# Earlier ring loads before a recurrent scan, and two of eight additions moved from VectorE to ScalarE and Pool after it

## The chip, the core and the metric

The kernel runs on one core of one Trainium2 chip. The metric is the device time of one execution in microseconds; lower is better. All data is float32.

## What is computed

The input x has 16 images of 128 channels and 64 x 64 pixels. Two layers follow each other, and each adds its result to its input:

```
x = x + lstm(gn(x))        # layer 0: gn = group norm over 32 groups of 4 channels
x = x + quantum(gn(x))     # layer 1

lstm:    skew the rows (row i shifted right by i), then scan over columns:
         gates = w_is @ x_t + w_ss0 @ h_of_the_row_above + w_ss1 @ h
         o, f, i = sigmoid(...); g = tanh(...)
         c = f*c + i*g;  h = o*tanh(c);  unskew h
quantum: per pixel: 4 angles = pre_w @ x + pre_b
         state of 4 qubits from cos/sin of the angles, a fixed circuit,
         z_w = sum of squared amplitudes with signs;  out = post_w @ z + post_b
```

## The kernel before

Channels are the 128 partitions. Forty of the 64 rows of all 16 images stay on chip in one tensor, `ring` (10 blocks of 4 rows per image); 24 rows have to be stored and read again, in a DRAM tensor `low`.

**Stage 1, loading and statistics (0 to 117 us).** A loop over the 16 images (line 360) issues on SP's queue two loads into `ring` (lines 362 to 366: 8 blocks and 2 blocks, 1 MB and 0.25 MB) and three loads of 0.25 MB for the other 24 rows into `rest` tiles (line 370; the pool has four buffers). VectorE (DVE) makes statistics pieces of 512 columns (line 373: five from `ring`, then three from `rest`) and one aggregate per image (line 374). Loads on SP and pieces on DVE are executed in the order of the program, so the loads of image b+1 stand behind the rest loads of image b, and a rest load waits until DVE has read the tile four loads before it. Beside this, on PE, ScalarE (ACT) and Pool, runs a chain of 27 small recurrent steps (`inv_step`, lines 184 to 204), which needs no image. When the last aggregate is there, mean and variance of the groups are made with two small matmuls and some operations of 16 columns, and the scan starts.

**Stage 2, the scan (117 to 1305 us).** PE-bound diagonal steps; the order of all engines is the order of the program. Rows that are finished are stored to `low` and replaced in `ring`. At its end the statistics of layer 1 are made.

**Stage 3, layer 1 (from 1320 us).** An image is eight chunks of 512 columns: k = 0 to 2 are low rows, loaded by Pool's queue (`load`, L741) into a pool with 11 buffers, k = 3 to 7 are views of `ring`. The order of every engine is again that of the program, over images b:

```
            load(b + 3)
            po = outputs(b, 0)
            finish(b, 0, po)
            angles(b + 2)
            po = outputs(b, 1)
            squares(b + 1)
            finish(b, 1, po)
```

`angles` makes phases with 16 matmuls that use the array in four column strips (theta, L752), adds a bias on ACT (y, L762), rounds and subtracts on DVE (L763, L764) and takes the sine on ACT in place (L765). The tile y has two buffers, so y of image b+2 takes the place of y of image b. `squares` multiplies the sines by amplitudes (am, L772) and squares them on ACT (sq, L774). `outputs` makes four products per half image in four row strips of the array (po, L781), each in a PSUM bank of its own; a bank has one buffer, so products of the next half wait until `finish` has read the bank. `finish` adds product, bias and input on DVE in place (L798), and SP's queue stores the chunks (L800 low rows, L803 ring rows).

PE executes phases, products and amplitude matmuls in this order: po of half 0 of b, theta of b+2, po of half 1 of b, am of b+1.

## Time and profile before

| | |
|---|---|
| median of three runs (lowest, highest) | 1481.57 us (1478.03, 1482.80) |
| the profiled execution, own time | 1480.57 us |
| its span from first to last instruction | 1478.8 us |
| last aggregate of stage 1 ends | 112.5 us |
| last of the 27 small steps (its copies on Pool end) | 102.4 us |
| first phases matmul of layer 1 | 1320.56 us |
| last addition of layer 1 ends | 1473.35 us |
| mean granted TensorE clock | 0.981 of full speed |

Busy time in the stage of layer 1 (1320 to 1479 us): the additions at L798 take 55.4 + 33.0 us on DVE (128 of them, 743 ns each when alone, 0.68 to 0.69 us apart when they follow one another), y, sine and squares 11.0 + 10.1 + 17.3 us on ACT; Pool issues low loads only (0.54 us each). A low-row load lands 3.7 us after its issue (median), a low-row store 5.2, a 1 MB ring load 8.0.

How to read it: the profile is of one execution. Its rows name the line of the kernel, the engine, the written and read tensors, the count and the busy time. "Idle before" is time in which the engine waited, with what ended the wait. SPq is the queue of transfers issued by SP. "Issue" in the chain of waits is time in which an engine waited for nothing that the profile shows.

### The profile page before, as it was taken

Reading aid. Unit: us, or ns where it says so; the run is one execution under the profiler, and the core shown is the slowest. Engines: PE = TensorE matmul, PEld = TensorE weight load, DVE = VectorE, ACT = ScalarE, POOL = GpSimd, SP = SyncE. Lnnn points to the kernel's source line nnn. Section 1 sums busy time; section 2 is a strip of 40 time slices with the busy share of each in tenths; the row PEclk is TensorE's granted clock in tenths of the full one; section 3 lists DMA queues with packets and bytes.
Section 4 is the critical chain, followed back from the end, with each engine's and each line's share of the span. In section 5 each row is a group of like instructions: output and inputs, shape, how many; then the busy total and the mean of one; then the engine's idle time right before and its main releaser. Section 6 shows DMA issues by size and latency. Waiting matters only on the chain. (4 is left out here: it accounts for less than half of the span.)

```text
span 1478.8 us, 19436 instructions
## 1 busy us (share of the span) xinstructions
PE 1374.0 (93%) x5798; PEld 973.1 (66%) x5798; DVE 976.4 (66%) x2458; ACT 764.6 (52%) x1862; POOL 889.8 (60%) x1694
## 2 busy tenths in 40 slices
PE   4647999999999999999999999999999999859997
PEld 3647888777677667667776776776677787833322
DVE  5884565556665666887777675555555678767775
ACT  3544566556555555555555555555555565432221
POOL 1114778766677667788887776676676666521110
PEclk9999999999999999999999999999999999979987
DMA  8990000000000000133344000000000000028997
GB/s 287 334 313 1 1 2 0 1 0 1 1 0 1 1 1 1 58 114 114 121 139 138 3 1 0 1 1 1 1 1 1 1 1 2 1 79 288 318 318 249
DMA packets 86192, 106.99 MB, mean 72 GB/s; under 512 B 4024, under 2 KB 70728, under 8 KB 86088
## 3 DMA queue, kind: packets, MB, share of 16 engines
q1 hardware_dynamic: 80576, 92.29, 18.3%
q0 software_dynamic: 3840, 12.59, 2.7%
q8 instruction: 46, 0.75, 0.2%
q10 hardware_dynamic: 1672, 0.89, 0.2%
q14 instruction: 58, 0.48, 0.1%
HBM read 59.61 MB, written 46.14 MB: 72 GB/s over the span
## 5 line engine op out<-in xcount | busy, mean ns | idle before, releaser
L483 PE MATMUL ps<-xn,wxT 128*128 128x512 f32 (+18 forms) x1280 | 480.7, 518 | 2.0 <-POOL xn L475 2.0
L596 DVE TENSOR_TENSOR ps<-ps,both 128x256 f32<-128x256 f32 (+9 forms) x544 | 219.7, 408 | 325.7 <-PE ps L574 320.1
L600 ACT ACTIVATE ps<-ps,bias 128x512 f32<-128x512 f32 (+23 forms) x480 | 268.3, 581 | 253.1 <-DVE ps L596 213.3
L483 PEld LDWEIGHTS ps<-xn,wxT 128*128 128x128 f32 x1280 | 231.9, 191 | 174.5 <-issue 155.5
L625 ACT COPY both<-ps 128x256 f32<-128x256 f32 (+9 forms) x544 | 191.4, 355 | 178.7 <-PE ps L574 159.0
L574 PE MATMUL ps<-diff,w1T 128*128 128x256 f32 (+14 forms) x1088 | 283.7, 363 | 0.0
L574 PE MATMUL ps<-diff,w0T 128*128 128x256 f32 (+14 forms) x1088 | 283.2, 362 | 0.0
L516 POOL TENSOR_TENSOR ring<-ring,hst 128x256 f32<-128x256 f32 (+8 forms) x488 | 247.2, 538 | 24.7 <-DVE hst L664 24.7
L574 PEld LDWEIGHTS ps<-hst,wsT 128*128 128x128 f32 x1088 | 195.9, 190 | 85.5 <-DVE hst L664 35.4
L574 PE MATMUL ps<-hst,wsT 128*128 128x256 f32 (+14 forms) x1088 | 241.3, 365 | 5.7 <-DVE hst L664 4.3
L574 PEld LDWEIGHTS ps<-diff,w0T 128*128 128x128 f32 x1088 | 199.7, 190 | 21.1
L574 PEld LDWEIGHTS ps<-diff,w1T 128*128 128x128 f32 x1088 | 199.3, 190 | 20.8
L475 POOL TENSOR_TENSOR xn<-xn,rstd 128x512 f32<-128x512 f32 (+10 forms) x160 | 170.7, 1067 | 15.2 <-DVE rstd L152 2.7
L470 POOL TENSOR_TENSOR xn<-ring 128x256 f32<-128x256 f32 (+8 forms) x213 | 146.9, 699 | 0.0
L664 DVE TENSOR_TENSOR hst<-g,ps 128x256 f32<-128x256 f32 (+13 forms) x320 | 108.4, 369 | 45.0 <-ACT g L655 41.8
L465 POOL TENSOR_TENSOR xn<-ring,mean 128x16 f32<-128x16 f32 (+8 forms) x247 | 130.3, 537 | 12.2 <-DVE mean L138 11.0
L655 ACT ACTIVATE g<-cst 128x256 f32<-128x256 f32 (+20 forms) x320 | 103.0, 368 | 63.8 <-DVE cst L654 63.3
L507 POOL TENSOR_TENSOR diff<-hst 128x240 f32<-128x240 f32 (+9 forms) x136 | 103.0, 757 | 39.0 <-DVE hst L664 35.6
L654 DVE TENSOR_TENSOR cst<-cst,ps 128x256 f32<-128x256 f32 (+20 forms) x320 | 104.6, 368 | 5.5
L651 DVE TENSOR_TENSOR ps<-ps,g 128x512 f32<-128x512 f32 (+20 forms) x160 | 95.2, 595 | 19.1 <-ACT g L600 17.8
L677 POOL COPY edge<-hst 128x16 f32<-128x16 f32 x64 | 25.1, 392 | 136.1 <-DVE hst L664 136.1
L644 DVE TENSOR_TENSOR cst<-cst,ps 128x512 f32<-128x512 f32 (+20 forms) x160 | 92.8, 580 | 16.8 <-ACT ps L600 9.4
(149 smaller groups left out, 1232.1 us busy)
## 6 DMA issues: line engine op xcount, KB each, us to landing
ring<-in_x_dram SPq DMA_DIRECT2D x16, 1024.0 KB, 8.0
out_dram<-ring SPq DMA_DIRECT2D x16, 1024.0 KB, 5.2
rest<-in_x_dram SPq DMA_DIRECT2D x48, 256.0 KB, 5.4
low<-ring SPq DMA_DIRECT2D x6, 2048.0 KB, 7.5
ring<-in_x_dram SPq DMA_DIRECT2D x6, 2048.0 KB, 8.2
low<-low POOLq DMA_DIRECT2D x48, 256.0 KB, 3.7
out_dram<-low SPq DMA_DIRECT2D x48, 256.0 KB, 5.2
ring<-in_x_dram SPq DMA_DIRECT2D x16, 256.0 KB, 8.1
```

Source lines behind the costliest of these rows:

```text
L465: nc.gpsimd.tensor_sub(by_pairs(xn, 0, j, n), x0, over(mean1, n))
L470: nc.gpsimd.tensor_sub(by_pairs(xn, 1, j, n), lower, of)
L475: nc.gpsimd.tensor_mul(v, v, r)
L483: nc.tensor.matmul(ps[g][:, :, a:b], lhsT=wxT[:, g * 128 : (g + 1) * 128], rhs=xns[t % 2][:, :, a:b], start=True, stop=True,)
L507: nc.gpsimd.tensor_sub(diff[:, 0, a1:b], now[:, 1, a1 - NB : b - NB], now[:, 0, a1:b])
L516: nc.gpsimd.tensor_add(x1, x1, by_pairs(new, q, j, n))
L574: nc.tensor.matmul(out, lhsT=w[:, g * 128 : (g + 1) * 128], rhs=rhs, start=False, stop=True, skip_group_check=True,)
L596: nc.vector.tensor_add(v, v, both[g][:, a:b])
L600: nc.scalar.activation(to[:, :, a:w], ps[g][:, :, a:w], FUNC[g], bias=bias[:, g : g + 1])
L625: nc.scalar.copy(both[g][:, a:b], ps[g][:, 0, a:b])
L654: nc.vector.tensor_add(c[:, q], c[:, q], ig[:, q])
L664: nc.vector.tensor_mul(new[:, q, a:v], th[:, q, a:v], act[GO][:, q, a:v])
```

## The change

Stage 1: the two ring loads of an image become a function `rows(b)`. Images 0 and 1 are loaded ahead of the loop, and iteration b loads the ring rows of image b+2 ahead of the rest tiles of image b.

Layer 1: in each half image the addition with j = 3 is split. ACT adds the bias and moves the product from PSUM to a new tile `part` (one buffer), and Pool adds it to the input in place. The pool of low rows gets a twelfth buffer. To make room, the square of half 1 is written into the y tile of its image in place of a tile of its own; both amplitude matmuls are issued ahead of both squares.

```diff
+            def rows(b):
                 n = SLOTS * NW
                 for k0, k1, at in ((AHEAD // ROWS, RING // ROWS, 0), (0, AHEAD // ROWS, n)):
                     nc.sync.dma_start(
                         out=ring[:, k0:k1, b, :],
                         in_=xv[b, :, at : at + (k1 - k0) * BLOCK].rearrange("c (k n) -> c k n", n=BLOCK),
                     )
+            rows(0)
+            rows(1)
+            for b in range(NB):
+                if b + 2 < NB:
+                    rows(b + 2)
                 of = [ring[:, k : k + 2, b, :] for k in range(0, RING // ROWS, 2)]
...
-    lowp = ctx.enter_context(tc.tile_pool(name="lowp", bufs=11))
+    lowp = ctx.enter_context(tc.tile_pool(name="lowp", bufs=12))
     trp = ctx.enter_context(tc.tile_pool(name="trp", bufs=2))
+    partp = ctx.enter_context(tc.tile_pool(name="partp", bufs=1))
...
     def squares(b):
         sqs[b] = []
+        ams = []
         for h in range(2):
             am = ps_a.tile([P, CHUNK], F32, name=f"am{b}_{h}", tag=f"am{h}")
             nc.tensor.matmul(am, lhsT=w_amp[:, h, :], rhs=turns[b], start=True, stop=True)
-            s = trp.tile([P, CHUNK], F32, name=f"sq{b}_{h}", tag=f"sq{h}")
+            ams.append(am)
+        for h, am in enumerate(ams):
+            s = trp.tile([P, CHUNK], F32, name=f"sq{b}", tag="sq") if h == 0 else turns[b]
             nc.scalar.activation(s, am, AF.Square)
             sqs[b].append(s)
...
-            nc.vector.scalar_tensor_tensor(x1, y, b_out, x1, ALU.add, ALU.add)
+            if j < 3:
+                nc.vector.scalar_tensor_tensor(x1, y, b_out, x1, ALU.add, ALU.add)
+            else:
+                part = partp.tile([P, CHUNK], F32, name=f"part{b}_{h}", tag="part")
+                nc.scalar.activation(part, po[j], AF.Identity, bias=b_out)
+                v = part
+                if k >= NT:
+                    v = v.rearrange("p (k n) -> p k n", n=BLOCK)
+                nc.gpsimd.tensor_add(x1, x1, v)
```

More of the change, by code (lines that the diff above doesn't have):

```diff
@@ L359 @@
             done = 0
-            for b in range(NB):
+            def rows(b):
                 n = SLOTS * NW
```

## The prediction

> **What bounds the kernel now.** I read the 40 slices first, then for each of the two changed stages the waits and the chain.

> ```profile
> PE   4647999999999999999999999999999999859997
> DVE  5884565556665666887777675555555678767775
> DMA  8990000000000000133344000000000000028997
> GB/s 287 334 313 1 1 2 0 1 0 1 1 0 1 1 1 1 58 114 114 121 139 138 3 1 0 1 1 1 1 1 1 1 1 2 1 79 288 318 318 249
> ```

> A slice is 37 us. There are three stages: loading with statistics (three slices, transfers at 8 to 9 tenths), the scan (PE at 9, nothing changed there), and layer 1 from 1320 us (PE and transfers both at 9). A gain in the first stage starts the scan earlier and is worth its full length.

> First stage: the waits of SP's queue up to 130 us, the waits of the engines up to 115 us, and three stretches (the last two columns are the share of the transfer engines and GB/s).

> ```profile
> SPq L370 <- DVE stats L373: 35.9, 29, 3.5
> SPq L370 <- DMA rest<-in_x_dram: 12.1, 12, 1.5
> ...
> DVE stats L373 <- DMA ring<-in_x_dram: 24.8, 15, 6.9
> ...
> 9.00:12.00 3.00, 0.49 (x1) 0.20 (x1) 2.04 (x9) 0.81 (x1) 0.00 (x0) 1.00 0.66 175
> 24.00:27.00 3.00, 1.87 (x8) 1.27 (x7) 2.96 (x7) 1.85 (x9) 0.58 (x3) 1.00 0.69 187
> 54.00:69.00 15.00, 9.85 (x44) 9.43 (x44) 12.66 (x23) 8.09 (x32) 3.02 (x16) 1.00 1.08 371
> ```

> DVE waits for ring rows, SP waits with its next load until DVE has read a rest tile, and so the transfers dip: 175 or 187 GB/s against 371 when nothing starves them. The mean from 2 to 108 us is 324.

> Layer 1: one image of the chain of waits, then the waits, then windows [...] (the clock is the column before the transfer share).

> ```profile
> 1396.16 0.70 ACT y L762
> ...
> 1396.88 0.71 DVE theta L763
> ...
> 1397.61 0.70 DVE y L764
> ...
> 1398.35 0.51 issue
> 1398.86 0.59 ACT sq L774
> 1399.45 0.04 issue
> 1399.49 2.68 PE po L781 x8
> 1402.17 3.60 PE theta L752 x16
> ...
> ACT y L762 <- PE theta L752: 77.6, 15, 6.6
> PEld theta L752 <- DMA low<-low: 5.7, 6, 1.3
> ...
> 1354.13:1357.54 3.41, 2.92 (x10) 1.05 (x8) 3.41 (x6) 1.36 (x3) 1.36 (x3) 1.00 0.80 245
> 1357.54:1360.95 3.41, 3.41 (x17) 0.60 (x16) 1.59 (x3) 0.00 (x0) 0.00 (x0) 0.50 0.93 327
> ```

> The chain closes on itself through PE, ACT and DVE: y, its rounding, its sine ("issue" 0.51), the squares, the output products, the next phases, the next y. With a full clock it takes 7.95 us (y at 1361.33 and 1369.28). From y of image 3 (1341.35) to y of image 15 (1453.20) there are 12 periods of 9.32 on average. Seven of them hold a half-clock stretch and average 9.87. Late low rows cost only 5.7 us of weight-load wait in all.

> [...] its half stretches last 3.41 us. But here the window before a half one isn't idle: it is PE busy 2.92 of 3.41, only with the quarter-array output products. In all seven cases the preceding window held those products and at most 0.5 us of other matmuls; with 0.6 us or more the clock stayed full. [...] The trace has 1067 ns for a 128x512 product on Pool (L475) and 580 to 595 on DVE. [...] y is an identity too, and it alternates with the sine with no load after 1318 us.

> **Part 1: ring rows two images ahead.** No instruction is added. On SP's queue 32 ring loads move ahead of the rest loads of two images. The lead keeps 1.3 MB or more queued while SP waits for DVE. Nothing else uses SP here except ACT's weight loads beside it, which share the transfer engines. It has a price: an image's last rest tile lands one 1.3 MB block later relative to the ring rows, so at the end DVE still has images 13, 14 and 15 to finish. Best case: 33.6 MB of x and 0.8 of weights, less the 2.4 of the three last rests, is 32.0 MB; at 0.371 MB/us (row 54:69) and 2.3 us of start that is 88.6 us; 0.7 for a rest tile; then DVE's pieces. From the timeline, five ring pieces take 3.06 us, three rest pieces 1.86, the aggregate 0.37: 2.2 for image 13 and 5.3 each for 14 and 15, 12.8 in all. End 102.1, where the profile has 112.5. DVE alone gives the same: its first rest tile lands at 2.3 + 5.5/0.371 = 17.1, then 2.2 + 15 x 5.3 + some 3 us of small operations, 101.8. Worst case: the mean rate of 30 to 105 us, 0.338, gives 110; delayed weight loads could eat the rest. The chain of 27 single-column steps (L184 to L204) ends at 102.4 and was hidden by 10 us; that cover goes, so it is late next. Gain from -1 to 10. I take 106, which allows for some dips and for the chain slipping: **-6.5 us**.

> **Part 2: layer 1.** Take s as the start of y (the activation at L762) of image b+2.

> Added wait. The second square now overwrites the y tile of image b, which the second output products of b read. There are two y tiles, so y of b+2 may be written only after those products, not after the phases. PE issues them right behind the phases: 1369.06 to 1370.20, and y would start 0.16 later, at 1370.36 instead of 1369.28: +1.08. Behind y on ACT wait its sine, both squares and the new activation; DVE's rounding waits too.

> Removed work. DVE does six additions instead of eight. Before: subtraction ends s+2.13, four additions of 0.68 to s+4.77, the last products (1.06 alone) end and the phases start at s+5.87. After: DVE's three end s+4.09. ACT has sine to 2.79, squares to 3.29 and 3.76, then the new activation, 0.58 like a pipelined y, to about 4.3. Products to 5.4: -0.47. The two matmuls ahead of both squares change nothing, since PE ran them before the squares already.

> Period: phases 5.4 to 7.26, second products to 8.36, y at **8.52** against 7.95.

> Pool. Per image two additions of 1.07 (bounds 0.59, DVE's price, and 1.3) and three issues of low loads, 1.65 together: 3.8 of 8.5 us, hidden. The load of b+4 is now queued behind the second addition of b (s+5.4). The twelfth buffer makes it need only image b's stores, which land near s+4, so it scarcely waits; the rows are needed near s+14 plus. Low waits (2.8 us within the 12 periods) go. On SP the stores of ring rows leave 0.7 to 1 us later, hidden except at the end.

> Clock. Between the end of the full-array products (L772) and the phases lay 3.07 us. Now those products end at s+1.93 and the phases start at 5.4: 3.47[...]. So windows with quarter-array work alone become more likely, and the half stretch then covers phases and second products, which are both on the chain: +1.71. 8.52 + 1.71 = 10.23 is three windows (10.24), so the next period meets the same window again: it locks. Forecast: 12 x 10.24 = 122.9 against 111.85, **+11.0**.

> Before those 12, y of image 2 waits for the second products of image 0, +1.3, and the next period +0.6: **+1.9**. End: from y of image 15, the products of image 14 no longer queue behind two of eight additions (L772 starts at s+7.6, not 9.46: -1.85), but the last addition is 0.65 on ACT plus 1.07 on Pool instead of 0.75, with one DVE turn saved: **-1.45**.

> Sum: -6.5 + 11.0 + 1.9 - 1.45 = **+5.0**. The profiled execution took 1480.57 (span 1478.8, 1.8 around it), 1.0 under the median of 1481.57; the difference put on the median gives 1486.5.

> **Rivals.**
> A, not slower: the clock doesn't lock. With n of 12 periods throttled layer 1 costs 12 x 8.52 + 1.71 n - 111.85 + 0.45, and the whole is -15.7 + 1.71 n. The point is n = 9: at 7, as now, -3.7 (1478); at 3, -10.5 (1471). For it: before, never more than three throttled periods in a row, and a spread from 9.33 to 10.37 us in them. Against: before, 9.87 wasn't a multiple of the window; 10.23 is.
> B, slower yet: the loads ahead bring nothing. SP already waited 12.1 us for earlier transfers to land (12 times), which may hold it again, or DVE's 12.8 us at the end take what the transfers give. Then +11.5: 1493. For it: DVE has 5.3 us of work per image against 5.75 of transfer. Against: the 371 GB/s stretch.
> C: Pool's queue, if stores land late. The load holds the addition behind it, and this holds ScalarE's single part tile: 0.5 us per image, +6 on top: 1492. Against: 4 us of slack.

> **Numbers.** Forecast 0.45, A 0.33, B and C 0.22. A change of 0.3% (4.4 us) is about what can be told from none. The forecast's own range, 1481 to 1491, gives 0.27 slower and 0.18 same; A 0.20 faster and 0.13 same; B and C 0.22 slower. Range 1473 to 1495.

> **What would show it.** First stage: the last aggregate at 106 (112.5 now), no 3 us stretch under 250 GB/s between 12 and 90 us, SP still waiting for DVE. Layer 1: ACT's y released by po (L781), no longer by theta; periods of 8.5 at full clock and 10.2 with a half stretch, eight or more of the latter; no theta wait on low. Pool's addition near 1.07. I am wrong if y starts while second products run, if layer 1's periods fall under 9.2, or if the scan's start moves by under 3 us.

## The result and the profile after

The changed kernel takes 1488.57 us (median of six runs, 1488.00 to 1490.19), the kernel before 1482.01 in the same comparison (also six runs): ratio 1.005, 95% interval 1.0037 to 1.0062. It is slower by 0.5%, on the forecast side; 1486.5 was predicted, with a range to 1495. The profiled execution took 1488.39 us, its span is 1486.6 (before: 1480.57 and 1478.8).

Lines of the page first: the same slices as before, then the new group.

```profile
PE   4658999999999999999999999999999998768886
DVE  6974565566656667877777765555555787755554
DMA  9970000000000000244431000000000000047877
GB/s 313 371 245 1 2 1 1 1 1 1 1 1 1 1 1 1 94 134 133 140 125 57 1 1 1 1 0 1 0 1 1 1 1 1 19 139 274 294 270 250
...
L820 POOL TENSOR_TENSOR ring<-ring,part 128x512 f32<-128x512 f32 x32 | 40.8, 1275 | 115.2 <-ACT part L816 115.1
```

The first two slices move more (313 and 371 GB/s for 287 and 334), so the third has less left to do. The slices of layer 1 move less (274 to 294 for 318) and PE falls to 8 tenths and below: layer 1 has become slower, and not for lack of transfers. An addition on Pool takes 1275 ns.

The first stage: waits of SP's queue up to 130 us, of DVE up to 115 us, and the stretch of 15 us that was the undisturbed one before, with three later ones. A line of waits gives the total in us, how often, and the longest. A line of a stretch gives its length, the busy time of PE, PE's weight loads, DVE, ACT and Pool (with the number of instructions), the granted clock, the share of the transfer engines and GB/s.

```profile
SPq L378 <- DVE stats L381: 27.3, 32, 4.6
SPq L378 <- DMA rest<-in_x_dram: 18.5, 14, 2.2
...
DVE stats L381 <- DMA ring<-in_x_dram: 12.6, 13, 6.9
...
54.00:69.00 15.00, 9.33 (x40) 8.90 (x40) 13.74 (x24) 8.07 (x32) 3.19 (x17) 1.00 1.06 366
93.00:96.00 3.00, 1.97 (x10) 1.89 (x10) 2.89 (x5) 1.54 (x6) 0.57 (x3) 1.00 0.73 279
96.00:99.00 3.00, 1.97 (x10) 1.89 (x10) 3.00 (x7) 1.54 (x6) 0.58 (x3) 1.00 0.63 194
99.00:102.00 3.00, 1.28 (x6) 1.19 (x6) 2.10 (x5) 2.27 (x7) 0.88 (x5) 1.00 0.75 230
```

SP still waits for DVE, but with ring rows queued that wait costs little: from 30 to 90 us the transfers run at 372 GB/s (339 before). From 93 us only rest tiles are left, one at a time behind DVE, and the rate falls. DVE is busy up to 100.4 us and then waits 1.2 us in all for the last rest tiles. The last aggregate ends at 104.0 us instead of 112.5, the 27 small steps end at 101.6, and y of image 0 starts at 1315.79 instead of 1324.23: 8.44 us earlier.

Layer 1: one period of the chain of waits, then the waits of the engines, and stretches of 3.41 us with the granted clock in each. "Half window" stands for such a stretch in which the granted clock is 0.50, "window" for any of them: in both profiles the steps of the clock in layer 1 lie whole multiples of 3.41 us apart (before, half windows start at 1347.30, 1357.54, 1401.91, 1412.15, 1422.39, 1439.46 and 1449.70).

```profile
1377.91 0.70 ACT y L771
...
1378.63 0.71 DVE theta L772
...
1379.42 0.70 DVE y L773
...
1380.15 0.63 ACT y L774
1380.78 0.49 ACT sq L787
1381.27 0.04 issue
1381.31 2.22 PE po L794 x8
1383.53 3.46 PE theta L761 x16
1386.99 1.19 PE po L794 x8
...
ACT y L771 <- PE po L794: 50.9, 14, 3.8
...
1379.93:1383.34 3.41, 2.03 (x8) 0.99 (x8) 3.03 (x6) 2.18 (x4) 0.94 (x1) 1.00 0.79 297
1383.34:1386.75 3.41, 3.41 (x17) 0.59 (x16) 1.20 (x2) 0.69 (x1) 3.17 (x5) 0.50 0.61 177
...
1390.17:1393.58 3.41, 1.96 (x8) 0.99 (x8) 3.03 (x6) 2.18 (x4) 0.87 (x1) 1.00 0.81 306
1393.58:1396.99 3.41, 3.41 (x18) 0.59 (x16) 1.26 (x2) 0.69 (x1) 3.23 (x5) 0.50 0.60 172
```

The second output products (1.19 us) now lie on the chain between the phases and the next y, and y's releaser is po where it was theta. The phases take 3.46 us instead of the 1.92 at a full clock (from 1322.88), because a half window (the 0.50) covers them. The half windows come one in every period: thirteen of them start from 1332.14 to 1455.02 us, 10.24 us apart, three windows. The window ahead of each holds output products and at most 0.32 us of phases or amplitude matmuls; every other window of these images has over 1.9 us of them. From the last amplitude matmul of an image to the next phases, with output products as the only matmuls between, it takes 3.7 to 4.2 us in these periods, 3.0 to 3.1 in most of before; the expectations below call this the stretch without full-array work. The twelve periods from y of image 3 to y of image 15 are all 10.30 to 10.34.

### The profile page after: what moved, and what is told of

Same layout as the page of the kernel before. It is cut to its first block, busy times and chain, and to the rows that moved or that the text cites. A ratio compares the mean times of both kernels' runs of the same rounds, so it can differ in the third digit from the quotient of the medians.

```text
span 1486.6 us, 19469 instructions
## 1 busy us (share of the span) xinstructions
PE 1371.5 (92%) x5798; PEld 973.2 (65%) x5798; DVE 955.4 (64%) x2426; ACT 784.6 (53%) x1894; POOL 929.9 (63%) x1726
## 5 line engine op out<-in xcount | busy, mean ns | idle before, releaser
L582 PEld LDWEIGHTS ps<-diff,w1T 128*128 128x128 f32 x1088 | 199.6, 191 | 20.5
L483 POOL TENSOR_TENSOR xn<-xn,rstd 128x512 f32<-128x512 f32 (+10 forms) x160 | 170.7, 1067 | 15.2 <-DVE rstd L152 2.7
L820 POOL TENSOR_TENSOR ring<-ring,part 128x512 f32<-128x512 f32 x32 | 40.8, 1275 | 115.2 <-ACT part L816 115.1
```

The source lines that it names most:

```text
L483: nc.gpsimd.tensor_mul(v, v, r)
L582: nc.tensor.matmul(out, lhsT=w[:, g * 128 : (g + 1) * 128], rhs=rhs, start=False, stop=True, skip_group_check=True,)
```

## The experiments

Times are medians; ratios are to the kernel before, run beside them. "Twelve periods" means the mean distance of y from image 3 to image 15 in the profiled execution: 9.32 us before, 10.31 after.

| kernel | us | ratio, 95% interval | twelve periods |
|---|---|---|---|
| after | 1488.57 | 1.0037 to 1.0062 | 10.31 |
| ring loads ahead alone | 1472.40 | 0.9914 to 0.9958 | 9.22 |
| layer 1 alone | 1496.23 | 1.0083 to 1.0137 | 10.28 |
| after, full-array filler | 1476.79 | 0.9956 to 0.9987 | 8.87 |
| after, small filler | 1488.13 | 1.0031 to 1.0063 | 10.22 |
| after, three y tiles | 1459.30 | 0.9823 to 0.9868 | 8.26 |
| after, additions on DVE | 1502.92 | 1.0124 to 1.0160 | 11.40 |
| after, two part tiles | 1488.94 | 1.0034 to 1.0066 | 10.31 |
| before, full-array filler | 1476.83 | 0.9954 to 1.0006 | 9.04 |
| three y tiles, additions on DVE | 1462.16 | 0.9850 to 0.9889 | 8.39 |
| ring loads one image ahead alone | 1469.03 | 0.9901 to 0.9949 | 9.51 |
| three y tiles, last image on DVE | 1457.98 | 0.9828 to 0.9872 | 8.31 |

### Each part alone

The first takes the statistics loop of after with layer 1 of before; the edit against before:

```diff
-            for b in range(NB):
+            def rows(b):
...
+            rows(0)
+            rows(1)
+            for b in range(NB):
+                if b + 2 < NB:
+                    rows(b + 2)
```

> Only the ring loads two images ahead; layer 1 as before. Theory (two separate effects that add): the scan starts 8.4 us earlier, as in the changed kernel, and everything after it is shifted: 8.4 us under before, 1473.6 us, layer 1's twelve periods still 9.3 on average. Rival (the earlier start only moves where layer 1 meets the windows of the clock, or is given back there): 1478 or more. A difference of under 5 us speaks for the rival.

Measured: 1472.40, 8.4 under before (1480.81 beside it). In its profile the last aggregate ends at 104.3 us, and the twelve periods average 9.22.

The reverse leaves the statistics loop of before and has all else of after; the edit against before, in part:

```diff
-    lowp = ctx.enter_context(tc.tile_pool(name="lowp", bufs=11))
+    lowp = ctx.enter_context(tc.tile_pool(name="lowp", bufs=12))
...
-            s = trp.tile([P, CHUNK], F32, name=f"sq{b}_{h}", tag=f"sq{h}")
+            s = trp.tile([P, CHUNK], F32, name=f"sq{b}", tag="sq") if h == 0 else turns[b]
...
+                nc.gpsimd.tensor_add(x1, x1, v)
```

> The changed layer 1 with the loads of the kernel before. Theory (the two parts add): before plus 8.4 (the first part undone) on the changed kernel, 1496 to 1498 us; y released by the second products, periods locked at 10.3. Rival (layer 1 is slow only because of where the earlier start put it against the clock's windows): under 1490 us.

Measured: 1496.23, 15.5 over before beside it (1480.73). The parts add: -8.4 and +15.5 make 7.1, and the whole change made 6.6. One expectation was wrong in form: periods weren't locked at 10.3 but alternated, 8.66 and 11.9, with the same mean. Two of them are 20.6 us, and pairs of half windows (6.8 us) lie 20.5 us apart. The periods of 8.66 meet no half window, those of 11.9 meet two, so the loss is nearly the same. The rival is out: layer 1 is slow without the earlier start too.

### The clock: an idle filler

```diff
+        nc.tensor.matmul(ths[b], lhsT=w_amp[:, 1, :], rhs=turns[b], start=True, stop=True)   # full
+        nc.tensor.matmul(ths[b][0:32, :], lhsT=w_amp[0:32, 1, 0:32],                         # small
+                         rhs=turns[b][0:32, :], start=True, stop=True, tile_position=(0, 0))
```

One or the other stands in `squares`, behind both amplitude matmuls and ahead of the squares; `ths[b]` is the phases bank of image b, which nobody reads any more. The small filler works 32 rows by 32 columns of the array, a sixteenth of it. It takes as long as the full one (600 and 593 ns on average).

> The changed kernel with one more full-array matmul (512 columns) per image right behind the amplitude matmuls, into a dead phases bank; its result is not used. Theory (the clock is halved in every period [...]): the stretch falls from 3.5 to 2.5 us, no half windows in the middle of layer 1, period 8.5 to 8.7 instead of 10.31, some 20 to 23 us less than the changed kernel: 1467 us. Rival (the period of 10.31 is the chain of the added wait and the slow Pool addition): more work on PE, period 10.3 or longer, 1488 to 1500 us.

> As the kernel with the full-array filler, but the extra matmul uses 32 rows and 32 columns of the array for the same time. If the clock follows how much of the array works: half windows stay in every period, 1486 to 1490 us. If it follows how long any matmul runs: like the full filler, 1467 us. If the chain is the cause: 1488 us or more.

The kernel with more work is faster: 1476.79 against 1488.57. Its profiled execution (1471.0 us) has no half window between 1318 and 1447 us. A stretch at the same times as the first pair's second window, in the kernel with the full filler, and then three neighbouring windows in the one with the small filler:

```profile
1383.34:1386.75 3.41, 3.41 (x24) 1.34 (x24) 2.78 (x5) 1.63 (x3) 2.30 (x3) 1.00 0.81 301
```

```profile
1395.30:1398.71 3.41, 3.41 (x23) 1.12 (x16) 0.66 (x2) 0.95 (x2) 2.37 (x4) 1.00 0.86 260
1398.71:1402.12 3.41, 2.74 (x9) 0.74 (x7) 3.11 (x5) 2.14 (x4) 0.00 (x0) 1.00 1.03 371
1402.12:1405.53 3.41, 3.41 (x14) 0.98 (x16) 2.16 (x3) 0.73 (x2) 2.30 (x3) 0.50 0.89 322
```

Both kernels issue the same number of matmuls in the same places; only how much of the array the filler uses differs. With the small one, PE is busy 2.74 of 3.41 and the next window is halved all the same. The twelve periods hold twelve half windows in after, eleven with the small filler and none with the full one. So in this pair a matmul of the same time took the half windows away when it used the full array (none in twelve periods) and left eleven when it used a sixteenth. The half windows are the reason why the period was 10.3 instead of 8.66: that is the commonest period with the full filler, and also the period of layer 1 alone, without any filler, where no half window falls. The expectation for the small filler was wrong in form: its half windows did not stay in every period. Most of its periods alternate between 8.66 and 11.9, as in layer 1 alone, with nearly the same mean. Whether the rows or the columns of the filler count, the pair doesn't tell.

The filler did not do it in every execution. No run reached the 1467 us that was expected; the 22 runs spread from 1470.07 to 1482.89, and the profiled one is among the fastest. The mean granted clock, on record for every run, shows why: the seven runs under 1474.5 us had 0.986 to 0.989, the ten over 1478 us 0.979 to 0.983, and over all of them time falls as the clock rises (correlation -0.98). A mean clock lower by 0.010 over 1480 us is about 30 us more at half clock, an estimate from these figures of some nine half windows. This points to half windows that came back in the slower executions; no profile shows where they fell.

### The wait: a third y tile

```diff
-        y = trp.tile([P, CHUNK], F32, name=f"y{b}", tag="y")
+        y = trp.tile([P, CHUNK], F32, name=f"y{b}", tag="y", bufs=3)
...
-            s = trp.tile([P, CHUNK], F32, name=f"sq{b}", tag="sq") if h == 0 else turns[b]
+            s = trp.tile([P, CHUNK], F32, name=f"sq{b}", tag="sq", bufs=1) if h == 0 else turns[b]
```

> The changed kernel with a third buffer for the y tile (room from one buffer less for the first square, which never has two alive), so that y of b+2 no longer waits for the second products of b. Theory (added wait, and the half clock that follows from it): y released by the phases, stretch without full-array work 2.6 us, period near 7.8, where the transfers end (2.88 MB per image at 0.371 MB/us): 12 periods save 30 us, 1459 us (1452 to 1466). Rival (the additions on ScalarE and Pool are what lengthens the period): 1484 us or more.

Measured: 1459.30, as expected to 0.3 us. (One buffer less for the first square has no part in it: the kernel with two part tiles below has that too and is no faster.) Two lines of its waits (y's releaser, and the new late one) and a window over its twelve periods:

```profile
ACT y L771 <- PE theta L761: 22.1, 12, 2.3
...
PEld theta L761 <- DMA low<-low: 8.3, 10, 1.1
...
1333.00:1431.00 98.00, 92.31 (x428) 29.72 (x424) 65.06 (x96) 41.97 (x71) 48.25 (x58) 1.00 1.02 353
```

Y is released by the phases again, no window is halved before 1447 us, and the transfers run at 353 GB/s, a share of 1.02, with the phases now waiting for low rows. That is the next bound: the shortest periods are 7.47 us, twelve of these would be 9.5 us less than the 99.1 measured, and the phases' waits for low rows come to 8.3.

### The additions

All eight sums back on DVE, the rest as after; then the same edit on the kernel with three y tiles:

```diff
-            if j < 3:
+            if j < 4:
```

> The changed kernel with all eight additions on VectorE again; the square in the y tile, the twelve buffers and the early ring loads stay, so the added wait stands alone. Theory: at a full clock the period is 7.95 + 1.08 = 9.0 us; the stretch without full-array work is 3.9 us, so nearly every period meets a half window and takes 10.7; that is 0.5 over three windows, so it can't stay locked and some periods run at 9.0. Mean of the twelve periods 10.0 to 10.8, total 1486 to 1495 us. Rival (the ScalarE and Pool additions are the loss, the wait is harmless): under 1478 us.

Measured: 1502.92, 8 above the upper end. None of the twelve periods ran at a full clock, so its price of 9.0 was not put to the test. The periods go 10.86, 10.86, 12.5 and again, 34.2 us in three, near ten windows of 3.41 (34.1). The expectation that it would fall out of step was wrong; it fell into a longer pattern. So the additions on ScalarE and Pool are not the loss: with the wait in place they save 14.4 us.

> As the kernel with three y tiles, but with all eight additions on VectorE: what the additions on ScalarE and Pool bring once the wait is gone. Theory: full-clock period 7.95 as before, with half windows again in some periods because the stretch is 3.1 us instead of 2.6; mean period 8.5 to 9.3, total 1462 to 1472 us, 4 to 12 above the kernel with three y tiles and the split additions. Rival (the split brings nothing, transfers bound both): within 3 us of it, 1459 us.

Measured: 1462.16; 2.9 above the three y tiles with split additions, whose interval overlaps. That is at the edge of the rival's range, but its reason holds for one of the two kernels only. The commonest period is 7.95 here, as in the kernel before at a full clock, and the shortest with the split is 7.47: the split takes 0.48 us off the chain. Here three of twelve periods take 9.4 to 9.65 with half windows, and the phases wait 0.3 us for low rows in all. With the split no period is halved, but the phases wait 8.3 us for low rows. So the transfers take back most of what the split wins.

> The changed kernel with two part tiles (room from one buffer less for the first square). Theory: ScalarE no longer waits for Pool's addition; at a full clock and at the end of the kernel this shows, but the twelve periods stay locked at 10.2 to 10.3 us because the clock's windows set them. From y of image 15 to the end 24 to 25 us instead of 26.3; total 1486 to 1488 us. Rival (the wait of ScalarE for Pool sets the period): periods fall by 0.5 us or more, under 1482 us.

```diff
-    partp = ctx.enter_context(tc.tile_pool(name="partp", bufs=1))
+    partp = ctx.enter_context(tc.tile_pool(name="partp", bufs=2))
```

(The first square has one buffer here too.) Measured: 1488.94, 0.9 above the expected range, periods 10.31, but from y of image 15 to the end still 26.26 us: expected was 24 to 25. The wait of ScalarE for Pool, 13.9 us in all of after, costs nothing while the half windows set the period; what it would cost at a full clock isn't known. The end is set elsewhere (below).

### The kernel before, and the best

The full filler in the kernel before, behind its squares:

```diff
             nc.scalar.activation(s, am, AF.Square)
             sqs[b].append(s)
+        nc.tensor.matmul(ths[b], lhsT=w_amp[:, 1, :], rhs=turns[b], start=True, stop=True)
```

> The kernel before, with one more full-array matmul per image behind the amplitude matmuls, its result not used. Theory: the seven half windows in the twelve periods of before go; each cost 1.9 us on average; the periods end at 8.0 to 9.0, held by late low rows (eleven buffers): 1466 to 1474 us. Rival (the transfers bound layer 1 before): 1478 us or more.

Measured: 1476.83, ratio 0.9954 to 1.0006: unclear by its interval, above the expected range. In the profile there is no half window between 1324 and 1457 us, so the filler did what it should, but the periods only fell from 9.32 to 9.04: phases wait for late low rows in place of the slow clock, 11.8 us between 1340 and 1450. As with the filler after, the slower of the seven runs had the lower clock (1487.29 us at 0.983, the profiled 1474.94 at 0.991). That the half windows and the late rows hid each other before is how I read the two numbers; no run took both away.

The ring loads ahead alone, with one image of lead; the edit against the same with two:

```diff
-            rows(1)
             for b in range(NB):
-                if b + 2 < NB:
-                    rows(b + 2)
+                if b + 1 < NB:
+                    rows(b + 1)
```

> Ring loads one image ahead instead of two, layer 1 as before. Theory (a lead of one block of 1.3 MB, 3.5 us of transfer, is all that has to bridge SP's wait for VectorE; the second image only delays the rest tiles by one more block at the end): at least as good as two images ahead, the last aggregate at 101 to 104 us where two ahead has 104.0, total 1470 to 1474 us. Rival (one block isn't enough and transfers dip again): last aggregate at 107 us or later, 1476 us or more.

Measured: 1469.03, 1.0 under the expected range, with the last aggregate at 104.3 us as with two images ahead alone. One image of lead is enough; the second brings nothing that shows. (Its profile has one period of 15.5 us, in which phases wait 6.1 for low rows.)

Three y tiles, and the last image's sums on DVE:

```diff
-            if j < 3:
+            if j < 3 or b == NB - 1:
```

> The kernel with three y tiles, and the additions of the last image all on VectorE: the candidate for the best. Theory: periods as with three y tiles (8.0 to 8.5, transfers full), the last addition no longer takes the way over ScalarE and Pool, 0 to 1.5 us less: 1458 us (1455 to 1461). Rival (the end is set by the last stores): no difference from 1459.3.

Measured: 1457.98, 1.3 under the three y tiles, with overlapping intervals: not told apart, and the end after y of image 15 takes 23.60 us in both, which speaks for the rival: the last addition comes 0.2 us earlier and the stores take that much longer. It is the fastest kernel here, 1.5% under before.

## Why the prediction was right, and where its terms were off

The direction, the mechanism and the size were right: a gain of the first stage, outweighed by a wait that puts the second products on the chain and by a half clock that then comes every period. The third y tile shows the wait with all that follows from it (29 us away, the half windows included), the pair of fillers shows the clock. The sum came close with some luck: the first stage brought 1.9 us more than predicted, and the other three terms cost 4.9 more.

| term | predicted | measured in the profiles |
|---|---|---|
| first stage | -6.5 | -8.44 |
| periods up to y of image 3 | +1.9 | 20.82 - 17.12 = +3.70 |
| twelve periods | +11.0 | 123.73 - 111.85 = +11.9 |
| from y of image 15 to the end | -1.45 | 26.28 - 25.57 = +0.7 |
| sum | +5.0 | +7.8 |

The last column compares two executions, and the medians are 6.6 apart.

*First stage.* The step "I take 106" was too careful. The end was 104.0, 1.9 over the best case of 102.1; 1.2 of these are DVE's waits for the last rest tiles. Single executions vary here: the last aggregate came at 110.6 to 112.5 in the three profiles with the old loads, and at 103.1 to 105.7 in the nine with ring loads two images ahead. The small steps, named as late next, ended at 101.6 and were never in the way. (The prediction's estimate by DVE alone takes 5.5 MB up to the first rest tile. Three ring blocks of 1.31, the tile of 0.26 and 0.8 of weights make 5.0, which is 1.3 us earlier; the 106 didn't rest on it.)

*First periods.* The first was +1.33 as worked out (7.80 for 6.47). The second was priced at full clock (+0.6) and was already halved: 10.31 for 7.95, +2.36.

*Twelve periods.* The full-clock period is 8.66, not 8.52. The shortest periods of the other kernels price its two steps: the split takes 0.48 off (7.95 to 7.47, -0.47 predicted), and the wait adds 1.19 (7.47 to 8.66, +1.08 predicted). With 1.65 for the half clock that is 10.31, not 10.23. "It locks" was right in effect and too strong as a word. The period (10.31) is 0.07 longer than the distance of the half windows (10.24): the first of the thirteen starts 0.32 us behind its phases, the last 1.02 ahead of them, and all thirteen lie on them. At which length of the stretch without full-array work the clock falls was not shown: seven of twelve periods hold a half window at mostly 3.0 to 3.1 us before, all twelve at 3.7 to 4.2 after. Without the earlier start the same kernel alternates between 8.66 and 11.9 and loses as much.

*The end.* The last addition came after 19.0 us for 20.15, a gain of 1.1 near the predicted 1.45. But the last stores were forgotten: from the last addition to the end of the span it took 7.3 us for 5.4. The 1 MB store has a 0.25 MB store and three low rows close ahead of it in SP's queue: it leaves 0.75 us after the last addition (0.03 before) and lands 5.6 us later (4.4 before).

*Pool.* The addition was sized at 1.07 and took 1.275, still inside the bounds given. That was a misread row: 1067 ns is the mean of L475 over products of different lengths (the page has "+10 forms" there). Its 128x512 products alone took as long as the addition, already in the kernel before:

```profile
L475 POOL TENSOR_TENSOR xn<-xn,rstd 128x512 f32<-128x512 f32 x100 | 127.0, 1270 | 7.8
```

The 580 and 595 ns for DVE are such means too; its 128x512 operations at L644 and L651 took 678 and 690. Pool's 1270 is 1.8 to 1.9 times that.

Rival A is refuted: the clock was not spared. Rival B is refuted: SP did wait 18.5 us for earlier transfers, but with ring rows queued the first stage still gained 8.4 us. Of rival C, the load no longer holds Pool up, and the wait for the part tile exists but two tiles change nothing. Of the signs named, two were missed: two stretches of 3 us between 21 and 27 us stayed at 249 and 237 GB/s, and Pool's addition was not near 1.07. The twelfth buffer of low rows had no run of its own: phases no longer wait for low rows after the change (5.7 us before), but the longer period alone could do that.

## What to carry to other kernels

## What the runs showed that was not expected

A matmul more per image made a kernel 11.8 us faster (1476.79 against 1488.57), and the same matmul on a sixteenth of the array made no difference that can be told (1488.13). With the same layer 1 the pattern of half windows repeated after 10.24 us (periods of 10.31) or after 20.5 (8.66 and 11.9), with the additions on DVE the periods repeated after 34.2 (10.86, 10.86, 12.5), and they stayed so from image 3 on; with the small filler the pattern changed from 20.5 to 10.24 on the way. One ring image of lead did as much as two. On Pool, an addition of two 128x512 tiles in place took 1275 ns, as long as a product of that size with a broadcast operand (1270).
